# Moving causal convolution taps from VectorE to TensorE in the opening of a mixed Mamba, attention and FFN kernel

## The chip, the cores and the metric

The kernel runs on one core of one Trainium2 chip. The metric is the device time of one execution in microseconds (us). Before the change the median of three executions is 5227.8 us (5223.77 to 5229.38). The core has five engines that run beside each other[...]: TensorE (PE in the profile; PEld is its weight load), VectorE (DVE), ScalarE (ACT), GpSimd (POOL) and SyncE (SP, which here only issues transfers). All data is float32.

## The reference, cut to what matters

The input has 8 batches of 384 channels on a 32 x 32 image, so 1024 positions. Layer 0 is a bidirectional Mamba block with a 3 x 3 depthwise convolution beside it; layer 1 is causal attention and a quantized feed-forward block. The change touches layer 0 alone:

```python
def mamba(x, in_proj_w, conv1d_w, conv1d_b, x_proj_w, dt_proj_w, dt_proj_b, A_log, D_param, out_proj_w):
    xz = jnp.einsum('blc,ec->ble', x, in_proj_w)
    u, z = jnp.split(xz, 2, axis=-1)
    uc = jax.lax.conv_general_dilated(u.transpose(0, 2, 1), conv1d_w[:, None, :], (1,), [(D_CONV - 1, 0)], ...,
                                      feature_group_count=C)          # 4 causal taps, each channel for itself
    u = silu((uc + conv1d_b[None, :, None]).transpose(0, 2, 1))
    x_dbl = jnp.einsum('blc,ec->ble', u, x_proj_w)
    dt, Bm, Cm = jnp.split(x_dbl, [dt_rank, dt_rank + D_STATE], axis=-1)
    delta = jax.nn.softplus(jnp.einsum('blr,dr->bld', dt, dt_proj_w) + dt_proj_b)
    A = -jnp.exp(A_log)
    deltaA = jnp.exp(delta[..., None] * A)
    deltaBu = (delta * u)[..., None] * Bm[:, :, None, :]
    def step(h, inp):
        dA, dBu, c = inp
        h = dA * h + dBu
        return (h, jnp.einsum('bdn,bn->bd', h, c))                    # 16 states for every channel
    _, ys = jax.lax.scan(step, h0, (...))
    y = (ys.transpose(1, 0, 2) + u * D_param) * silu(z)
    return jnp.einsum('bld,od->blo', y, out_proj_w)

fwd = mamba(x_flat, *mparams)
bwd = jnp.flip(mamba(jnp.flip(x_flat, axis=1), *mparams), axis=1)
conv = jax.lax.conv_general_dilated(x_norm, dw_w[:, None, :, :], (1, 1), [(1, 1), (1, 1)], ...)
local_feat = jax.nn.sigmoid(conv + dw_b[None, :, None, None]) * x_norm
x = x + res_scale * ((fwd + bwd) * scale_mod + local_feat)
# layer 1: attention, then a feed-forward block with binarized weights w1, w2
```

## The kernel before

Channels lie on the 128 partitions in three groups `c`; positions lie along a row in two halves `h` of 512. Both directions `d` use the same `up`, the unconvolved projection. Everything of one batch that must be there before the recurrence is made by `before_scan`. It appends small steps to a list `emit`; for the first batch a second list, `later`, takes what the recurrence doesn't need at once.

```python
PARTS = ((0, 0), (0, 1), (1, 1), (1, 0))      # (direction, half), in the order of the recurrence
BANKS = {"y": 1, "da": 2, "s": 2, "pt": 2, "av": 1}      # the 8 banks of PSUM by use
# pools: "big" has 6 buffers of 128 x 3072, "mid" has 10 of 128 x 1024

def before_scan(b, tags, emit, later=None):
    ...                                        # load x, normalize it into st["xn"]
    def in_proj(c, i, h):                      # i = 0: up, i = 1: z
        mp = bank_of(f"in_{b}_{c}_{i}_{h}")
        for k in range(NC):
            nc.tensor.matmul(out=mp, lhsT=st["win", c][:, k, i, :], rhs=st["xn"][:, k, half(h)], ...)   # L337
        nc.scalar.copy(st["up" if i == 0 else "z", c][:, half(h)], mp)                                  # L344

    def conv(c, d, h):
        acc = bank_of(f"u{d}_{b}_{c}_{h}")
        up = st["up", c]
        for s in range(DCONV):
            w = vec[:, c, V_CW + DCONV - 1 - s : V_CW + DCONV - s]
            if s == 0:
                nc.scalar.activation(acc, up[:, half(h)], AF.Copy, scale=w)                             # L353
                continue
            ...                                # tap: up shifted by s, to: where it lands
            nc.vector.scalar_tensor_tensor(to, tap, w, to, ALU.mult, ALU.add)                           # L363
        nc.scalar.activation(st["u", d, c][:, half(h)], acc, AF.Identity, bias=vec[:, c, V_CB : V_CB + 1])  # L364

    def local(c, h): ...                       # 3 x 3 taps: one on ACT (L374), eight on DVE (L384)

    for c in range(NC):
        ...                                    # buffers for up, z and both u; weights of group c + 1
        for i in range(2):
            for h in range(NH):
                emit(lambda c=c, i=i, h=h: in_proj(c, i, h), 2.6)
        for d in range(2):
            for h in range(NH):
                emit(lambda c=c, d=d, h=h: conv(c, d, h), 3.0)
        ...
        if later is None:
            emit(gates, 14.0)                  # silu of both u and of z, local taps, tanh (L384, L424, L443 to L453)
        else:
            emit(gates_of_us, 4.0)             # silu of both u
            later(gates, 10.0)
        ...                                    # project: x_proj on TensorE (L477), summed into xd on DVE (L488)

    def delta(c, d, h):
        ...                                    # softplus: TensorE (L508), four on ACT (L511 to L514)
        nc.vector.scalar_tensor_tensor(dl, dp, 0.0, dl, ALU.max, ALU.add)                               # L515
        nc.vector.scalar_tensor_tensor(dp, w, 1.0, e, ALU.subtract, ALU.subtract)                       # L516
        nc.vector.tensor_tensor(dl, dl, dp, ALU.subtract)                                               # L517
        nc.vector.tensor_tensor(u, u, dl, ALU.mult)                                                     # L518
        ...                                    # both results go to DRAM

    for c in range(NC):
        for d, h in PARTS:
            emit(lambda c=c, d=d, h=h: delta(c, d, h), 3.0)
```

The recurrence is cut into 768 units, 96 for each batch: a part (direction and half), a channel group and two of the 16 states. Within a part the first eight states of groups 0, 1, 2 come first, then the other eight of groups 2, 1, 0. One unit is:

```python
def s_first(u):  # two units ahead
    pin(nc.gpsimd.tensor_tensor(g, ud, bc_row_B, ALU.mult))                          # L578, 128 x 1024
def s_scan(u):
    for i in range(2):
        nc.scalar.activation(da, dl, AF.Exp, scale=amat[:, u.c, n : n + 1])          # L591
        nc.vector.tensor_tensor_scan(gi, da, gi, first, ALU.mult, ALU.add)           # L596
    if begins:
        pin(nc.gpsimd.tensor_copy(carry[:, u.n : u.n + 2], g[:, :, end]))            # L601
    pin(nc.gpsimd.tensor_tensor(g, g, bc_row_C, ALU.mult))                           # L602
def s_sum(u):    # one unit behind: eight 128 x 128 transposes that add up in one bank of PSUM
    nc.tensor.matmul(out=y[:, j, :], lhsT=g[:, i, chunk(j)], rhs=ident, is_transpose=True, ...)  # L610
```

The opening is put together so, with batches in the order 0, 1, 2, 3, 5, 6, 4, 7:

```python
first = slots(-AHEAD - 2, per + 1)             # the recurrence of the first batch
before_scan(ORDER[0], ("s", "pt"), begin, beside)
run(begin)                                     # alone
beside += steps_of(before_scan, ORDER[1], ("s", "pt"))
beside += steps_of(binarize, w1, w1s, NC, FF, 2, "w1")
beside += steps_of(binarize, w2, w2s, NF, C, 8, "w2")
for b in ORDER[2 : 1 + ahead]:                 # the third and fourth batch
    beside += steps_of(before_scan, b, ("s", "pt"))
run(first, beside)                             # spread evenly beside those 96 units
...                                            # then attention and FFN of the batches beside the other units
```

The order in which steps are written is a wish: a scheduler fixes the queue of every engine when the kernel is built, and may move an instruction ahead when it takes its inputs to be ready.

Of the kernel before, what the change touches and what calls it, by code (L numbers as in the profile page):

```python
# [12 lines left out]
ALU = mybir.AluOpType  # L13
# [4 lines left out]
P = 128  # L18
B, C, H, W = 8, 384, 32, 32
L = H * W  # L20
NC = C // P
# [5 lines left out]
DCONV = 4  # L27
# [13 lines left out]
PARTS = ((0, 0), (0, 1), (1, 1), (1, 0))  # L41
# [3 lines left out]
ORDER = (0, 1, 2, 3, 5, 6, 4, 7)  # L45
# [3 lines left out]
V_NORM, V_CW, V_CB, V_DTB, V_D, V_DW, V_DWB, V_BP, V_B2, V_ALOG = 0, 1, 5, 6, 7, 8, 17, 18, 19, 20  # L49
# [4 lines left out]
def kernel(  # L54
# [16 lines left out]
    nc = tc.nc  # L71
# [14 lines left out]
    def btile(name):  # L86
        return big.tile([P, NC, L], F32, name=name, tag="big")

    def mtile(name, n=L):
        return mid.tile([P, n], F32, name=name, tag="mid")  # L90
# [212 lines left out]
                    )  # L303


    def before_scan(b, tags, emit, later=None):

        st = {}
        turns = itertools.cycle(tags)

        def bank_of(name):
            return bank(name, next(turns))
# [19 lines left out]
                    )  # L332

        def in_proj(c, i, h):
            mp = bank_of(f"in_{b}_{c}_{i}_{h}")
            for k in range(NC):
                nc.tensor.matmul(  # L337
                    out=mp,
                    lhsT=st["win", c][:, k, i, :],
                    rhs=st["xn"][:, k, half(h)],  # L340
                    start=(k == 0),
                    stop=(k == NC - 1),
                )
            nc.scalar.copy(st["up" if i == 0 else "z", c][:, half(h)], mp)  # L344

        def conv(c, d, h):

            acc = bank_of(f"u{d}_{b}_{c}_{h}")
            up = st["up", c]
            for s in range(DCONV):  # L350
                w = vec[:, c, V_CW + DCONV - 1 - s : V_CW + DCONV - s]
                if s == 0:
                    nc.scalar.activation(acc, up[:, half(h)], AF.Copy, scale=w)  # L353
                    continue
                lo, hi = h * HB, (h + 1) * HB
                if d == 0:
                    t0, t1 = max(lo, s), hi
                    tap = up[:, t0 - s : t1 - s]
                else:
                    t0, t1 = lo, min(hi, L - s)  # L360
                    tap = up[:, t0 + s : t1 + s]
                to = acc[:, t0 - lo : t1 - lo]
                nc.vector.scalar_tensor_tensor(to, tap, w, to, ALU.mult, ALU.add)  # L363
            nc.scalar.activation(  # L364
                st["u", d, c][:, half(h)], acc, AF.Identity, bias=vec[:, c, V_CB : V_CB + 1]
            )

        def local(c, h):

            acc = bank_of(f"loc_{b}_{c}_{h}")  # L370
            r0, rows = h * (HB // W), HB // W
            img = acc.rearrange("p (i j) -> p i j", j=W)
            src = st["xn"][:, c, :].rearrange("p (i j) -> p i j", j=W)
            nc.scalar.activation(  # L374
                acc, st["xn"][:, c, half(h)], AF.Copy, scale=vec[:, c, V_DW + 4 : V_DW + 5]
            )
            for k in range(9):
                di, dj = k // 3 - 1, k % 3 - 1
                if k == 4:
                    continue  # L380
                i0, i1 = max(r0, -di), min(r0 + rows, H - di)
                j0, j1 = max(0, -dj), W - max(0, dj)
                to = img[:, i0 - r0 : i1 - r0, j0:j1]
                nc.vector.scalar_tensor_tensor(  # L384
                    to,
                    src[:, i0 + di : i1 + di, j0 + dj : j1 + dj],
                    vec[:, c, V_DW + k : V_DW + k + 1],
                    to,
                    ALU.mult,
                    ALU.add,  # L390
                )
            return acc

# [10 lines left out]
        for c in range(NC):  # L404

            @emit
            def _(c=c):
                st["up", c] = mtile(f"up_{b}_{c}")
                st["z", c] = mtile(f"z_{b}_{c}")
                for d in range(2):  # L410
                    st["u", d, c] = mtile(f"u{d}_{b}_{c}")
                if c + 1 < NC:
                    weights_of(c + 1)

            for i in range(2):
                for h in range(NH):
                    emit(lambda c=c, i=i, h=h: in_proj(c, i, h), 2.6)
            for d in range(2):
                for h in range(NH):
                    emit(lambda c=c, d=d, h=h: conv(c, d, h), 3.0)  # L420

            def silus(ts):
                for t in ts:
                    pin(nc.scalar.activation(t, t, AF.Silu))  # L424

            def sum_of_us(c=c):
                usum = mtile(f"us_{b}_{c}")
                nc.vector.tensor_tensor(usum, st["u", 0, c], st["u", 1, c], ALU.add)
                spill((b, "us", c), usum, f"sus_{b}_{c}")
                for d in range(2):  # L430
                    spill((b, "u", d, c), st["u", d, c], f"su_{d}_{b}_{c}")


            def gates(c=c, silus=silus, sum_of_us=sum_of_us):
                st["xc"] = mtile(f"xc_{b}_{c}")
                load(st["xc"], x[b, chunk(c), :])
                accs = [local(c, h) for h in range(NH)]
                with tc.high_priority(offset=60):
                    us = [st["u", 0, c], st["u", 1, c]] if later is None else []
                    silus(us + [st["z", c]])  # L440
                    for h in range(NH):
                        pin(
                            nc.scalar.activation(  # L443
                                accs[h], accs[h], AF.Tanh, scale=0.5, bias=dwbh[:, c : c + 1]
                            )
                        )
                    pin(nc.scalar.preload_act_table_set(LOG_EXP))
                for h in range(NH):
                    acc, xc = accs[h], st["xc"][:, half(h)]
                    nc.vector.scalar_tensor_tensor(  # L450
                        acc, acc, 1.0, st["xn"][:, c, half(h)], ALU.add, ALU.mult
                    )
                    nc.vector.scalar_tensor_tensor(xc, acc, rsh, xc, ALU.mult, ALU.add)  # L453
                spill((b, "t", c), st["xc"], f"st_{b}_{c}")
                spill((b, "z", c), st["z", c], f"sz_{b}_{c}")
                if later is None:
                    sum_of_us()

            def gates_of_us(c=c, silus=silus, sum_of_us=sum_of_us):
                with tc.high_priority(offset=60):  # L460
                    silus([st["u", 0, c], st["u", 1, c]])
                    pin(nc.scalar.preload_act_table_set(LOG_EXP))
                sum_of_us()

            if later is None:
                emit(gates, 14.0)
            else:
                emit(gates_of_us, 4.0)
                later(gates, 10.0)


            for h in range(NH):

                def project(c=c, h=h):
                    xp = bank_of(f"xp_{b}_{c}_{h}")
                    for d in range(2):
                        nc.tensor.matmul(  # L477
                            out=xp[d * DW : (d + 1) * DW, :],
                            lhsT=wx[:, c, :],
                            rhs=st["u", d, c][:, half(h)],  # L480
                            start=True,
                            stop=True,
                        )
                    xd = st["xd"][:, half(h)]
                    if c == 0:
                        nc.scalar.activation(xd, xp, AF.Identity, bias=onerow)
                    else:
                        nc.vector.tensor_tensor(xd, xd, xp, ALU.add)  # L488

                emit(project)  # L490
# [30 lines left out]
                nc.sync.dma_start(out=t, in_=du[:, i, :])  # L521
                spilled[b, what, d, c, h] = t

        for c in range(NC):
            for d, h in PARTS:
                emit(lambda c=c, d=d, h=h: delta(c, d, h), 3.0)


# [560 lines left out]
        for f, _ in spread_over(*lists):  # L1089
            f()  # L1090

    def steps_of(stage, *args):
        out = Steps()
        stage(*args, out)
        return out


# [1 line left out]
    per, ahead = len(units) // B, 3  # L1099
    first = slots(-AHEAD - 2, per + 1)  # L1100
    others = slots(per + 1, len(units) + 1)
    beside = Steps()
    begin = Steps()
    before_scan(ORDER[0], ("s", "pt"), begin, beside)
    run(begin)
    beside += steps_of(before_scan, ORDER[1], ("s", "pt"))
    beside += steps_of(binarize, w1, w1s, NC, FF, 2, "w1")
    beside += steps_of(binarize, w2, w2s, NF, C, 8, "w2")
    for b in ORDER[2 : 1 + ahead]:
        beside += steps_of(before_scan, b, ("s", "pt"))  # L1110
    run(first, beside)

    rest, later, due = [], list(ORDER[1 + ahead :]), [(0.0, 0)]
# [74 lines left out]
```

## Time and profile before

| | us |
|---|---|
| median of three executions | 5227.8 |
| span of the profiled execution | 5226.4 |
| PE busy | 4198.9 (80%) |
| DVE busy | 3630.7 (69%) |
| ACT busy | 2738.5 (52%) |
| POOL busy | 3680.7 (70%) |
| first POOL instruction of the recurrence (L578) starts | 133.90 |
| 192nd scan of 1536 (L596), the last of the first batch, lies between | 815 and 820 |
| last POOL instruction of the recurrence (L602) starts | 4942.6 |

Busy times say how long each engine had something under way, over the whole span. The opening, up to about 815 us, has another mix of work than the rest, and is to be read from its own stretch. The column PEclk is the clock that TensorE was granted, as a share of its full speed[...].

### The profile page before, as it was taken

What the parts mean: (1) busy time and instruction counts of PE and PEld (TensorE: products, weight loads), DVE (VectorE), ACT (ScalarE), POOL (GpSimd) and SP (SyncE); (2) the same over time, 40 slices, a digit from 0 to 9 for tenths busy, and PEclk for the clock granted to TensorE, in tenths of its full rate; (3) what the DMA queues carried; (4) which work ended last, traced back from release to release, by engine and by line L of the source; (5) the groups of instructions that cost most, each with busy time, mean ns of one, the idle gap of its engine ahead of it and who ended that gap; (6) DMA issues with size and microseconds to landing.
All of it is one profiled execution on the core that took longest, in us unless ns stands there. A gap on an engine that the chain in (4) does not pass through costs nothing.

```text
span 5226.4 us, 50586 instructions
## 1 busy us (share of the span) xinstructions
PE 4198.9 (80%) x16554; PEld 2222.6 (43%) x16554; DVE 3630.7 (69%) x4313; ACT 2738.5 (52%) x4934; POOL 3680.7 (70%) x1932
## 2 busy tenths in 40 slices
PE   5455667888878888788887888978888888988799
PEld 2233333444434444444443444434444444544444
DVE  6998998667776667876677856678766655565522
ACT  4665564555644556545556445565464454463334
POOL 0477777887679776787776788677888877787600
PEclk7667677889988899888898889988999989999899
DMA  6544545324463234543244632335433234224200
GB/s 228 210 164 156 184 166 196 109 84 149 143 205 105 91 110 161 169 158 119 97 139 133 213 123 91 108 128 201 141 119 130 89 101 158 85 77 151 83 30 25
DMA packets 365007, 696.35 MB, mean 133 GB/s; under 512 B 30104, under 2 KB 88904, under 8 KB 364744
## 3 DMA queue, kind: packets, MB, share of 16 engines
q1 hardware_dynamic: 355232, 676.97, 38.3%
q10 hardware_dynamic: 9512, 16.15, 0.9%
q8 instruction: 131, 2.15, 0.2%
q14 instruction: 132, 1.08, 0.1%
HBM read 527.33 MB, written 165.68 MB: 133 GB/s over the span
## 4 chain that ended last, share of the span: by engine, by line
POOL 35%; PE 21%; issue 16%; DVE 15%; ACT 4%; DMA 1%; POOLq 0%; SPq 0%; DVEq 0%; ACTq 0%
POOL g L578 18%; POOL g L602 17%; DVE g L596 6%; PE y L610 3%; PE qp L715 3%; PE yp L1015 2%; PE av L854 2%; PE s L770 2%; PE ap L911 2%; DVE loc L384 2%; PE pt L842 1%; DVE dp L516 1%; DVE u L363 1%; PE hp L970 1%; DVE du L518 1%
## 5 line engine op out<-in xcount | busy, mean ns | idle before, releaser
L578 POOL TENSOR_TENSOR g<-ud,bc 128x1024 f32<-128x1024 f32 x768 | 1834.5, 2389 | 730.6 <-PE y L610 579.9
L602 POOL TENSOR_TENSOR g<-g,bc 128x1024 f32<-128x1024 f32 x768 | 1819.8, 2370 | 277.6 <-DVE g L596 215.5
L591 ACT ACTIVATE da<-dl,amat 128x512 f32<-128x512 f32 x1536 | 1057.5, 691 | 1572.1 <-DVE g L596 1530.2
L610 PE MATMUL y<-ident,g 128*128 128x128 f32 x6144 | 969.2, 307 | 403.1 <-POOL g L602 337.6
L596 DVE TENSOR_TENSOR_SCAN g<-da,carry,g 128x512 f32<-128x512 f32 x768 | 954.9, 1271 | 460.2 <-POOL g L578 413.2
L596 DVE TENSOR_TENSOR_SCAN g<-da,g 128x512 f32<-128x512 f32 x768 | 906.5, 1209 | 508.5 <-POOL g L578 483.0
L610 PEld LDWEIGHTS y<-ident,g 128*128 128x128 f32 x6144 | 798.8, 158 | 837.3 <-POOL g L602 504.1
L770 PE MATMUL s<-k,q 64*128 64x512 f32 (+3 forms) x1152 | 469.9, 606 | 166.0 <-ACT pr L790 143.7
L789 DVE TENSOR_REDUCE nm<-s 128x1 f32<-128x512 f32 (+3 forms) x576 | 300.4, 545 | 251.0 <-PE s L779 182.5
L790 ACT ACTIVATE pr<-s,nm 128x512 f32<-128x512 f32 (+3 forms) x576 | 329.4, 575 | 149.5 <-DVE nm L789 148.4
L854 PE MATMUL av<-ptn,v 128*64 128x512 f32 (+3 forms) x1152 | 376.5, 556 | 24.8 <-DVE o L866 24.3
L970 PE MATMUL hp<-t,w 128*128 128x512 f32 x720 | 339.4, 615 | 33.2 <-ACT h L978 10.6
L842 PE MATMUL pt<-ident,pr 128*128 128x128 f32 x1728 | 312.3, 302 | 46.8 <-ACT ptn L844 24.3
L337 PE MATMUL in<-xn,win 128*128 128x512 f32 x576 | 301.2, 665 | 57.2 <-DVE xn L330 16.6
L1015 PE MATMUL yp<-h,w 128*128 128x512 f32 x720 | 330.5, 617 | 10.9 <-DMA w<-w2s 10.9
L844 ACT COPY ptn<-pt 128x512 f32<-128x512 f32 (+3 forms) x576 | 261.8, 480 | 128.8 <-PE pt L842 127.5
L770 PEld LDWEIGHTS s<-k,q 64*128 64x128 f32 x1152 | 163.3, 207 | 332.6 <-ACT pr L790 214.1
L842 PEld LDWEIGHTS pt<-ident,pr 128*128 128x128 f32 x1728 | 209.0, 152 | 180.7 <-ACT ptn L844 82.0
L715 PE MATMUL qp<-t,wqk 128*128 128x512 f32 x576 | 268.0, 616 | 22.0 <-DVE t L301 16.5
L601 POOL COPY carry<-g 128x2 f32<-128x2 f32 x384 | 84.4, 220 | 255.5 <-DVE g L596 255.5
L384 DVE SCALAR_TENSOR_TENSOR loc<-xn,vec,loc 128x496 f32<-128x496 f32 (+3 forms) x384 | 254.6, 721 | 4.3 <-ACT loc L374 4.0
L363 DVE SCALAR_TENSOR_TENSOR u<-up,vec,u 128x512 f32<-128x512 f32 (+3 forms) x288 | 201.5, 743 | 30.8 <-ACT u L353 30.4
(156 smaller groups left out, 4695.0 us busy)
## 6 DMA issues: line engine op xcount, KB each, us to landing
bc<-rows SPq DMA_DIRECT2D x512, 512.0 KB, 4.0
dl<-sdl SPq DMA_DIRECT2D x160, 256.0 KB, 2.8
ud<-sud SPq DMA_DIRECT2D x160, 256.0 KB, 2.7
t<-st SPq DMA_DIRECT2D x63, 512.0 KB, 5.1
su<-u SPq DMA_DIRECT2D x48, 512.0 KB, 5.2
du<-su SPq DMA_DIRECT2D x96, 256.0 KB, 4.5
sdl<-du SPq DMA_DIRECT2D x96, 256.0 KB, 2.7
sud<-du SPq DMA_DIRECT2D x96, 256.0 KB, 2.4
```

The costliest lines, as they stand in the source:

```text
L384: nc.vector.scalar_tensor_tensor(to, src[:, i0 + di : i1 + di, j0 + dj : j1 + dj], vec[:, c, V_DW + k : V_DW + k + 1], to, ALU.mult, ALU.add,)
L578: pin(nc.gpsimd.tensor_tensor(g, ud, sst["bc", 0, u.b, u.part, u.n], ALU.mult))
L591: nc.scalar.activation(da, sst["dl", u.b, u.c, u.part], AF.Exp, scale=amat[:, u.c, n : n + 1])
L596: nc.vector.tensor_tensor_scan(gi[:, ::step], da[:, ::step], gi[:, ::step], first, ALU.mult, ALU.add)
L602: pin(nc.gpsimd.tensor_tensor(g, g, sst["bc", 1, u.b, u.part, u.n], ALU.mult))
L610: nc.tensor.matmul(out=y[:, j, :], lhsT=g[:, i, chunk(j)], rhs=ident, is_transpose=True, start=(u.opens and i == 0 and j == 0), stop=(u.cl ...
L715: nc.tensor.matmul(out=qp, lhsT=st["wqk"][:, c, o : o + P], rhs=st["xn"][:, c, half(h)], start=(c == 0), stop=(c == NC - 1),)
L770: nc.tensor.matmul(out=ss[e][:, : k1 - k0], lhsT=st["q"][rows_of(e), c, chunk(qi)], rhs=st["k"][rows_of(e), c, k0:k1], start=True, stop=(k ...
L842: nc.tensor.transpose(pt[:, chunk(i)], pr[:, e, chunk(j % QT)], ident)
L854: nc.tensor.matmul(out=av[rows_of(e), cols], lhsT=st["v"][:, j, hd * HD : (hd + 1) * HD], rhs=st["ptn", j, e][:, cols], start=(j % QT == 0 ...
L970: nc.tensor.matmul(out=hp, lhsT=st["w1"][:, c, chunk(m % 2)], rhs=st["xn"][:, c, half(h)], start=(c == 0), stop=(c == NC - 1),)
L1015: nc.tensor.matmul(out=yp, lhsT=st["w2", k // 6][:, k % 6, :], rhs=st["h", k // NC][:, k % NC, half(h)], start=(k == 0), stop=(k == NF - 1),)
```

## The change

Three things change, all in the opening. They are for taking work off VectorE while the batches 1, 2 and 3 are prepared beside the first recurrence, and for letting that recurrence begin sooner.

The batches 1, 2 and 3 get their four causal taps as four matmuls that add up in one bank of PSUM. The weight of each is a diagonal matrix with the taps of 128 channels on its diagonal. The twelve diagonals are made once, on GpSimd, from the identity, and lie in one of the six "big" buffers until the last of these convolutions. The first batch and the four later ones (5, 6, 4, 7) keep their taps on ACT and DVE.

The z projections of the first batch go from the part that runs alone to the list beside the recurrence; their weights are held until then, and the buffer of z is taken only when it is made.

The deltas of each batch are made by direction and half first and channel group second, in the order in which the recurrence asks for them.

```diff
-    def before_scan(b, tags, emit, later=None):
+    def before_scan(b, tags, emit, later=None, diags=None):
...
         def in_proj(c, i, h):
+            if i == 1 and h == 0:
+                st["z", c] = mtile(f"z_{b}_{c}")
...
-                w = vec[:, c, V_CW + DCONV - 1 - s : V_CW + DCONV - s]
-                if s == 0:
+                k = V_CW + DCONV - 1 - s
+                w = vec[:, c, k : k + 1]
+                if s == 0 and diags is None:
                     nc.scalar.activation(acc, up[:, half(h)], AF.Copy, scale=w)
                     continue
...
-                nc.vector.scalar_tensor_tensor(to, tap, w, to, ALU.mult, ALU.add)
+                if diags is None:
+                    nc.vector.scalar_tensor_tensor(to, tap, w, to, ALU.mult, ALU.add)
+                else:
+                    nc.tensor.matmul(
+                        out=to,
+                        lhsT=diags(c, k),
+                        rhs=tap,
+                        start=(s == 0),
+                        stop=(s == DCONV - 1),
+                        skip_group_check=True,
+                    )
...
-                st["z", c] = mtile(f"z_{b}_{c}")
...
-            for i in range(2):
+            for i, to in enumerate((emit, emit if later is None else later)):
                 for h in range(NH):
-                    emit(lambda c=c, i=i, h=h: in_proj(c, i, h), 2.6)
+                    to(lambda c=c, i=i, h=h: in_proj(c, i, h), 2.6)
...
-        for c in range(NC):
-            for d, h in PARTS:
+        for d, h in PARTS:
+            for c in range(NC):
                 emit(lambda c=c, d=d, h=h: delta(c, d, h), 3.0)
...
+    taps = btile("taps").rearrange("p c l -> p (c l)")[:, : NC * DCONV * P]
+    taps = taps.rearrange("p (c k q) -> p c k q", c=NC, k=DCONV)
+    for c in range(NC):
+        for k in range(DCONV):
+            nc.gpsimd.tensor_scalar(
+                taps[:, c, k, :], ident, vec[:, c, V_CW + k : V_CW + k + 1], None, ALU.mult
+            )
...
-    beside += steps_of(before_scan, ORDER[1], ("s", "pt"))
+    beside += steps_of(before_scan, ORDER[1], ("s", "pt"), diags=diags)
...
-        beside += steps_of(before_scan, b, ("s", "pt"))
+        beside += steps_of(before_scan, b, ("s", "pt"), diags=diags)
```

More of the change, by code (lines that the diff above doesn't have):

```diff
@@ L383, in local @@
                 to = img[:, i0 - r0 : i1 - r0, j0:j1]
+                tap = src[:, i0 + di : i1 + di, j0 + dj : j1 + dj]
                 nc.vector.scalar_tensor_tensor(
[L385 to L390, printed above, removed]
+                    to, tap, vec[:, c, V_DW + k : V_DW + k + 1], to, ALU.mult, ALU.add
                 )
@@ L1090, in run, with steps_of @@
             f()
-    def steps_of(stage, *args):
+    def steps_of(stage, *args, **kwargs):
         out = Steps()
-        stage(*args, out)
+        stage(*args, out, **kwargs)
         return out
@@ L1101, with diags @@
     others = slots(per + 1, len(units) + 1)
+    taps = btile("taps").rearrange("p c l -> p (c l)")[:, : NC * DCONV * P]
[5 more added lines that the diff above has]
+            )
+    def diags(c, k):
+        return taps[:, c, k - V_CW, :]
     beside = Steps()
```

## The prediction

> **What bounds the kernel now.** I read the stretches first, because the shares of the whole span mix two regimes. I cut the span at four places: the first POOL instruction of the recurrence (133.90 us), the twelfth scan (222 us, at the end of a long wait of POOL), and the 192nd scan (815 us), which ends the first batch. The columns are busy us and count for PE, PEld, DVE, ACT and POOL, then granted clock, DMA share and GB/s.
>
> ```profile
> 0.00:134.00 134.00, 67.22 (x130) 26.43 (x130) 83.77 (x130) 64.56 (x88) 1.44 (x13) 0.73 0.65 229
> ...
> 134.00:222.00 88.00, 30.98 (x66) 14.55 (x67) 86.33 (x111) 51.75 (x75) 34.00 (x18) 0.56 0.60 216
> 222.00:815.00 593.00, 373.66 (x1141) 197.15 (x1139) 542.35 (x636) 368.10 (x549) 429.21 (x221) 0.69 0.51 173
> 815.00:5226.00 4411.00, 3727.07 (x15219) 1984.48 (x15218) 2918.24 (x3438) 2254.10 (x4224) 3216.05 (x1681) 0.90 0.37 123
> ```
>
> From 134 to 815 us DVE is the bound: 86 of 88 us, then 542 of 593 us (91%). From 815 us on it is busy for 66% only and TensorE for 84%, at clock 0.90. What the change takes from DVE can therefore only count in the 593 us; in the 88 us no tap is run.
>
> Next the groups of instructions in 134 to 806 us: busy us and mean ns, then idle time of the engine before them and what ended it.
>
> ```profile
> L578 POOL TENSOR_TENSOR g<-ud,bc 128x1024 f32<-128x1024 f32 x97 | 236.3, 2437 | 132.7 <-DMA sdl<-du 132.0 <-DMA ud<-sud 0.7
> L602 POOL TENSOR_TENSOR g<-g,bc 128x1024 f32<-128x1024 f32 x94 | 222.4, 2366 | 85.9 <-DVE g L596 65.9 <-issue 16.2
> L610 PE MATMUL y<-ident,g 128*128 128x128 f32 x749 | 147.5, 362 | 187.3 <-POOL g L602 185.7 <-DVE yt L629 1.1
> L384 DVE SCALAR_TENSOR_TENSOR loc<-xn,vec,loc 128x465 f32<-128x465 f32 (+3 forms) x192 | 126.1, 720 | 0.1
> L363 DVE SCALAR_TENSOR_TENSOR u<-up,vec,u 128x512 f32<-128x512 f32 (+3 forms) x108 | 75.1, 741 | 1.4 <-ACT u L353 1.2
> L516 DVE SCALAR_TENSOR_TENSOR dp<-ew 128x512 f32<-128x512 f32 x37 | 58.3, 1584 | 0.2
> L353 ACT ACTIVATE u<-up,vec 128x512 f32<-128x512 f32 x36 | 24.1, 682 | 0.0
> ```
>
> The reader sees that the taps never wait (1.4 us before 108 of them), that POOL waits for scans, and that TensorE waits 187 us for POOL: there is room on it. Last the timeline of TensorE at two places, which gives the price of a matmul at either clock.
>
> ```profile
> 430.23 1.02 PE L337 MATMUL in<-xn,win 128*128 128x512 f32 x2
> 433.92 1.09 PE L610 MATMUL y<-ident,g 128*128 128x128 f32 x8 [2.66 <-POOL g L602]
> ...
> 552.01 1.97 PE L610 MATMUL y<-ident,g 128*128 128x128 f32 x8 [2.93 <-POOL g L602]
> ```
>
> [...] the eight transposes of a unit take 1.97 us when they stand alone and 1.09 us behind matmuls, and the opening[...] has clock 0.69 where the rest has 0.90. [...]
>
> **The change part by part.**
>
> Taps off DVE: 108 instructions, 75.1 us busy. A row of them is spaced by 0.67 us (six in 4.02 us), so 72 us are freed. 36 first taps leave ACT, 24.1 us, where 368 of 593 us were busy: nothing for the end.
>
> Taps onto TensorE: 3 batches x 12 accumulators x 4 = 144 matmuls. One float32 matmul is two instructions in this trace (L337 counts 576 for 288), and twelve of them at full clock take 5.15 us (rows of L715 in the chain of waits), 0.43 each. So 144 x 2 x 0.43 = 124 us at full clock. What is there now is 373.66 x 0.69 = 258 us at full clock; the 18 z matmuls of the first batch, which come over, add 18 x 0.86 = 15. Sum 397 us at full clock: 441 us at 0.90, 496 at 0.80, 575 at 0.69, against DVE at 542 - 75 = 467 and POOL at 429. Three engines are then nearly level where one stood out.
>
> Because [...] a unit may run only two or three units ahead, I take the maximum by stretch, not over the whole. One channel group of one batch takes 8 units of the recurrence. Before, on DVE: 12 taps 8.0, 16 local taps 10.2, four more of the gates 2.7, sum of u 1.4, two sums of xd 1.3, 16 scans at 1.23 makes 19.7; together 43.3 us. POOL: 8 x (2 x 2.36 + 0.19) = 39.3 us. TensorE at full clock: four projections 10.3, x_proj 2.7, transposes 8 x 1.09 = 8.7; 21.7 us. DVE bounds it, at 43.3. The stretch of deltas takes 12 x (0.67 + 1.58 + 0.67 + 1.11) = 48 us and 13 scans, 64 us, all DVE. Nine groups and three stretches of deltas give 9 x 43.3 + 3 x 64 = 582 us, with 15 us for normalization 597, against 593 in the trace: the sum holds.
>
> After: DVE 43.3 - 8.0 = 35.3; POOL 39.3; TensorE 21.7 + 16 x 0.86 = 35.5 at full clock, 39.4 at 0.90, 44.4 at 0.80, 51.4 at 0.69. The deltas stay at 64. A group therefore goes from 43.3 to 39.4 at clock 0.90: 9 x 3.9 = 35 us, not 72, because POOL's recurrence stands right below DVE. I choose 0.90 since TensorE will now be busy as densely as in the rest. Of the 35 us I take half, 18 us: where three engines are level, [...] the copy of a finished convolution (L364) stands ahead of the exponentials that the next scans need, and now it waits for TensorE.
>
> z projections: 6 accumulators x 2.57 us leave TensorE before the recurrence, but beside the DVE taps of the same group, not in front of them. Their ACT copies push the third and fourth first tap back, for which DVE waited 0.24 us in the first group. I give it 3 us over three groups.
>
> Order of the deltas: three deltas, not one, are ready when the first unit starts. But from 134 to 222 us DVE is busy for 98%, with all twelve deltas and the local taps of the first batch to do in any order. It brings nothing there by itself. The queues of the changed build also put the sums of w1 ahead of the first normalization, which costs some 6 us at first, and spare the later convolutions the same interleaved sums; I count 2 us in favour over the 134 us. Start: -3 - 2 = -5 us.
>
> The twelve diagonals are 128 x 128 on an idle POOL before 134 us; nothing. The queues after the first 96 units hold the same work in nearly the same order, so the rest keeps its 4411 us and a gain of the opening passes through to the end.
>
> Sum: 5228 - 18 - 5 = 5205 us.
>
> **The rivals.**
>
> TensorE becomes the bound at a low clock. At 0.69 a group would take 51.4 us, 9 x 8.1 = 73 us more than before: 5228 + 73 - 5 = 5296. [...] Against it: the stretch 815 to 5226 us, as dense as this would be, has 0.90.
>
> DVE stays the bound and the whole relief comes through. 75.1 / 0.914 = 82 us: 5228 - 82 - 5 = 5141. For it: DVE's 91% and the taps' idle time of nearly nothing. Against it: 39.3 us of POOL in each group, which a faster DVE cannot go below.
>
> The waits cancel everything. If the ACT queue waits for convolutions, the scans come late and DVE idles where it worked: about 5225. For it: ACT already waited for TensorE before the copies of up (24.0 us in this stretch). Against it: ACT is 62% busy there.
>
> The taps' buffer. One of six big buffers is held, so the image of the third batch may load later. That wait was not on the path, as loads of x were far ahead of their use; some 5 us at the most.
>
> **Range and chances.** The clock carries the range. At 1.00 the group is bound by POOL at 39.3, so 36 us in full and 5 at the start make 5187; a looser tie between POOL and DVE could bring another 20 to 30. At 0.80 a group takes 44.4, 10 us in all against it: 5233, with waits about 5245. So 5160 to 5250 should hold it 8 times in 10. Faster by over 2% needs 105 us, more than the 82 of the second rival and the start together: 0.05. Slower by over 2% needs the low clock and more: 0.03. Within 2%: 0.92.
>
> **What would show it.** Each step has its place in the profile of the changed kernel. The first POOL instruction of the recurrence should start near 129 us. Between the twelfth and the 192nd scan I expect some 575 us in place of 593, with DVE near 470 us busy (about 82%), TensorE near 440 at a clock of about 0.9, POOL still 429. The groups should show 288 matmuls for the taps in place of L363's 108. The time after the 192nd scan should be 4411 us within 20. I am wrong if the clock of that stretch stays near 0.7 (first rival), if DVE is still above 90% busy there (second), if ACT's idle time before the copies of the convolutions exceeds some 40 us (third), or if the time after the first batch changes by more than the opening.

## The result and the profile after

The changed kernel takes 5201.86 us (median of four executions, 5197.06 to 5212.38) against 5225.78 us before (5217.87 to 5229.38). The ratio is 0.9959, with a 95% interval of 0.9939 to 0.9979: 24 us faster, about 0.5%. In a second measurement with 22 executions the ratio is 0.9965 (0.9955 to 0.9975).

First the same stretches as before, cut at the first instruction of the recurrence on GpSimd (129.50 us), at the scan that ends GpSimd's long wait (217.20 us; here it is the ninth, before the change it was the twelfth) and at the first scan of the second batch (808.90 us). The columns are busy us and count for PE, PEld, DVE, ACT and POOL, then granted clock, DMA share and GB/s.

```profile
0.00:129.50 129.50, 52.40 (x94) 19.07 (x94) 83.71 (x131) 61.82 (x82) 8.33 (x24) 0.72 0.65 228
129.50:217.20 87.70, 50.51 (x95) 21.10 (x96) 87.10 (x108) 50.74 (x75) 29.49 (x15) 0.66 0.65 228
217.20:808.90 591.70, 460.70 (x1447) 229.36 (x1445) 486.13 (x543) 357.24 (x525) 443.09 (x227) 0.82 0.52 176
808.90:5195.00 4386.10, 3703.95 (x15208) 1967.51 (x15208) 2910.46 (x3427) 2248.25 (x4217) 3209.95 (x1679) 0.91 0.37 124
```

The prediction put the end of the first batch at 815 us. The last of its scans begins at 819.59 us, and the first of the second batch at 827.42 us, so here is the kernel before once more, from its twelfth scan to the first of the second batch, and below it the changed kernel between the same two scans.

```profile
221.50:827.40 605.90, 380.94 (x1159) 200.79 (x1157) 555.25 (x646) 377.73 (x565) 439.40 (x225) 0.69 0.51 174
220.60:808.87 588.27, 457.85 (x1440) 228.40 (x1440) 482.70 (x540) 355.40 (x522) 442.18 (x226) 0.82 0.52 176
```

VectorE is relieved of 73 us in that stretch (555 to 483) and is now busy for 82% of it in place of 92%. TensorE takes on 77 us at a clock that rises from 0.69 to 0.82. Yet the stretch shrinks by 18 us only. The groups of the changed kernel from 217 to 809 us show where TensorE and GpSimd stand (busy us and mean ns, then idle time before them).

```profile
L587 POOL TENSOR_TENSOR g<-ud,bc 128x1024 f32<-128x1024 f32 x91 | 224.5, 2467 | 26.7 <-PE y L619 26.6
L611 POOL TENSOR_TENSOR g<-g,bc 128x1024 f32<-128x1024 f32 x92 | 218.2, 2372 | 69.1 <-DVE g L605 47.0 <-DMA sud<-du 14.6 <-issue 4.1
L370 PE MATMUL u<-up,taps 128*128 128x512 f32 (+3 forms) x288 | 128.7, 598 | 0.0
L605 DVE TENSOR_TENSOR_SCAN g<-da,carry,g 128x512 f32<-128x512 f32 x96 | 119.2, 1270 | 42.0 <-POOL g L587 37.5 <-ACT da L600 4.4
L605 DVE TENSOR_TENSOR_SCAN g<-da,g 128x512 f32<-128x512 f32 x89 | 104.0, 1208 | 36.1 <-POOL g L587 32.1 <-ACT da L600 4.0
L378 ACT ACTIVATE u<-u,vec 128x512 f32<-128x512 f32 x36 | 23.4, 671 | 0.0
```

The 288 instructions of the taps (L370) cost 128.7 us, and none waits. The copy of a finished convolution (L378) doesn't wait either. What is new stands before the scans: VectorE waits for GpSimd's L587. The view of the waits gives the sum, first of the kernel before (221 to 827 us), then of the kernel after (217 to 809 us): us in total, times, longest.

```profile
POOL carry L601 <- DVE g L596: 115.7, 12, 45.5
POOL g L602 <- DVE g L596: 74.9, 12, 10.4
...
DVE g L596 <- POOL g L578: 12.2, 11, 2.5
```

```profile
POOL carry L610 <- DVE g L605: 99.4, 8, 49.0
DVE g L605 <- POOL g L587: 69.6, 37, 2.5
...
POOL g L611 <- DVE g L605: 47.0, 7, 18.8
```

The longest wait in the first line of either view (45.5 and 49.0 us) is the long one that ends where the stretch begins. VectorE's wait for GpSimd grew from 12.2 to 69.6 us, by 57 us. That is most of the 73 us that it was relieved of. How it looks in time: the timelines of VectorE and of GpSimd in the changed kernel, at the beginning of the preparation of batch 1, where no tap is left on VectorE.

```profile
221.72 2.31 DVE L605 TENSOR_TENSOR_SCAN g<-da,g 128x512 f32<-128x512 f32 x2
224.60 2.34 DVE L605 TENSOR_TENSOR_SCAN g<-da,g 128x512 f32<-128x512 f32 x2 [0.57 <-POOL g L587]
229.47 2.34 DVE L605 TENSOR_TENSOR_SCAN g<-da,g 128x512 f32<-128x512 f32 x2 [2.53 <-POOL g L587]
```

```profile
222.21 2.35 POOL L587 TENSOR_TENSOR g<-ud,bc 128x1024 f32<-128x1024 f32 x1
224.51 0.18 POOL L610 COPY carry<-g 128x2 f32<-128x2 f32 x1
224.77 2.35 POOL L611 TENSOR_TENSOR g<-g,bc 128x1024 f32<-128x1024 f32 x1
227.07 2.36 POOL L587 TENSOR_TENSOR g<-ud,bc 128x1024 f32<-128x1024 f32 x1
229.36 0.20 POOL L610 COPY carry<-g 128x2 f32<-128x2 f32 x1
```

GpSimd works without a gap, 4.87 us for a unit, and VectorE has two scans in that time and nothing else to do. Why it has nothing else to do stands in the timelines of TensorE and ScalarE.

```profile
234.94 3.59 PE L370 MATMUL u<-up,taps 128*128 128x512 f32 x8
240.46 0.69 ACT L600 ACTIVATE da<-dl,amat 128x512 f32<-128x512 f32 x1 [3.07 <-DVE g L605]
...
245.34 0.69 ACT L600 ACTIVATE da<-dl,amat 128x512 f32<-128x512 f32 x1 [3.07 <-DVE g L605]
246.45 0.69 ACT L600 ACTIVATE da<-dl,amat 128x512 f32<-128x512 f32 x1 [0.42 <-DVE g L605]
247.08 0.67 ACT L378 ACTIVATE u<-u,vec 128x512 f32<-128x512 f32 x1
```

The first convolution is finished on TensorE at about 238.5 us. Its copy stands in ScalarE's queue behind exponentials (L600) of the recurrence, which come at GpSimd's pace, and starts only at 247.08 us. ScalarE is idle twice for 3.07 us around that time, until a scan of VectorE ends, and the copy, whose input is finished within the first of these waits, isn't taken ahead of the exponentials.

The pace of a channel group can be read at the instruction that adds both u, one for each group (L428 before, L437 after). Between these additions of one batch lie 43.3 us on average before the change (36.7 to 47.3, six intervals) and 40.2 us after (36.8 to 43.7).

### The profile page after: what moved, and what is told of

Read it like the earlier page. It is cut to its first block, busy times and chain, and to the rows that moved or that the text cites. A ratio compares the mean times of both kernels' runs of the same rounds, so it can differ in the third digit from the quotient of the medians.

```text
span 5195.3 us, 51029 instructions
## 1 busy us (share of the span) xinstructions
PE 4267.6 (82%) x16842; PEld 2237.0 (43%) x16842; DVE 3567.4 (69%) x4205; ACT 2718.1 (52%) x4898; POOL 3690.9 (71%) x1944
## 4 chain that ended last, share of the span: by engine, by line
POOL 38%; PE 20%; DVE 17%; issue 16%; ACT 6%; DMA 3%; POOLq 0%; SPq 0%; ACTq 0%; DVEq 0%
POOL g L587 19%; POOL g L611 18%; DVE g L605 6%; PE qp L724 3%; PE y L619 3%; PE av L863 2%; PE s L779 2%; PE yp L1024 2%; PE ap L920 2%; DVE loc L399 2%; DVE dp L525 2%; PE pt L851 1%; DVE u L368 1%; DVE du L527 1%; PE op L694 1%
## 5 line engine op out<-in xcount | busy, mean ns | idle before, releaser
L587 POOL TENSOR_TENSOR g<-ud,bc 128x1024 f32<-128x1024 f32 x768 | 1837.1, 2392 | 729.7 <-PE y L619 576.5
L600 ACT ACTIVATE da<-dl,amat 128x512 f32<-128x512 f32 x1536 | 1058.6, 692 | 1614.3 <-DVE g L605 1574.0
L619 PE MATMUL y<-ident,g 128*128 128x128 f32 x6144 | 926.1, 298 | 273.6 <-POOL g L611 211.8
L619 PEld LDWEIGHTS y<-ident,g 128*128 128x128 f32 x6144 | 769.4, 153 | 695.3 <-POOL g L611 328.4
L1024 PEld LDWEIGHTS yp<-h,w 128*128 128x128 f32 x720 | 139.7, 198 | 176.9 <-issue 166.4
```

The costliest lines, as they stand in the source:

```text
L587: pin(nc.gpsimd.tensor_tensor(g, ud, sst["bc", 0, u.b, u.part, u.n], ALU.mult))
L600: nc.scalar.activation(da, sst["dl", u.b, u.c, u.part], AF.Exp, scale=amat[:, u.c, n : n + 1])
L1024: nc.tensor.matmul(out=yp, lhsT=st["w2", k // 6][:, k % 6, :], rhs=st["h", k // NC][:, k % NC, half(h)], start=(k == 0), stop=(k == NF - 1),)
```

## The experiments

All ratios are against the kernel before, on the same chip and beside it. The last two columns are read from the traces: when the recurrence starts on GpSimd, and when the second batch's first scan starts.

| run | median us | ratio (95% interval) | start | second batch |
|---|---|---|---|---|
| before (its first profile) | 5225.78 | | 133.9 | 827.4 |
| changed kernel (its first profile) | 5201.86 | 0.9959 (0.9939 to 0.9979) | 129.5 | 808.9 |
| after_again | 5213.26 | 0.9965 (0.9955 to 0.9975) | 128.5 | 804.9 |
| taps_only | 5211.10 | 0.9959 (0.9948 to 0.9970) | 140.1 | 807.5 |
| order_only | 5239.28 | 1.0009 (0.9998 to 1.0019) | 134.1 | 830.4 |
| z_only | 5228.65 | 0.9994 (0.9979 to 1.0008) | 123.9 | 802.7 |
| taps_doubled | 5269.13 | 1.0071 (1.0057 to 1.0085) | 129.0 | 846.4 |
| one_tap | 5212.25 | 0.9956 (0.9939 to 0.9972) | 128.2 | 802.0 |
| deltas_beside_next | 5214.93 | 0.9969 (0.9957 to 0.9981) | 129.3 | 810.1 |
| deltas_and_gates_spread | 5210.59 | 0.9963 (0.9950 to 0.9976) | 129.1 | 807.6 |
| last_deltas_in_rest | 5205.10 | 0.9952 (0.9935 to 0.9968) | 130.0 | 757.5 |
| last_deltas_in_rest_late_gates | 5204.75 | 0.9952 (0.9937 to 0.9967) | 128.7 | 756.8 |
| last_deltas_in_rest_taps_on_vector | 5224.05 | 0.9984 (0.9969 to 0.9998) | 124.5 | 796.7 |
| half_of_second_multiply | 5152.31 | 0.9839 (0.9816 to 0.9862) | 130.5 | 747.4 |

### Which part carries the gain

The first four runs take the change apart. Two theories stood against each other: the gain lies in the taps, or it lies in the start (the z projections and the order of the deltas), for the first 24 units end 20 us earlier in the changed kernel (319 in place of 339 us) than before.

The changed kernel itself, as a yardstick:

> The changed kernel as it is, as a yardstick for the single parts. Both theories: 20 to 30 us under the kernel before, ratio 0.994 to 0.996.

The taps alone. The edit takes back the other two parts:

```diff
-        for d, h in PARTS:
-            for c in range(NC):
+        for c in range(NC):
+            for d, h in PARTS:
                 emit(lambda c=c, d=d, h=h: delta(c, d, h), 3.0)
...
-            for i, to in enumerate((emit, emit if later is None else later)):
+            for i in range(2):
                 for h in range(NH):
-                    to(lambda c=c, i=i, h=h: in_proj(c, i, h), 2.6)
+                    emit(lambda c=c, i=i, h=h: in_proj(c, i, h), 2.6)
```

> The kernel before with the taps of batches 1, 2 and 3 on TensorE and nothing else changed. Theory 1 (the gain lies in the taps, bounded by GpSimd and TensorE): 15 to 22 us under the kernel before; the time between the twelfth scan and the end of the first batch shorter by that much, VectorE near 490 us busy there, TensorE's clock above 0.8. Theory 2 (the gain lies in the start: z and the order of the deltas): within 6 us of the kernel before.

The order of the deltas alone, on the kernel before (the first hunk above, the other way round):

> The kernel before with only the order of the deltas changed. Theory 1: within 4 us of the kernel before, since VectorE is busy for 98% around the first units and has all twelve deltas to do in either order. Theory 2: 8 to 20 us faster, and the first part of the recurrence (24 units) ends some 15 us earlier, as it does in the changed kernel (319 for 339 us).

The z projections alone, on the kernel before (the second hunk, the other way round, with the buffer of z taken when it is made):

> The kernel before with only the z projections of the first batch moved beside the recurrence. Theory 1: 0 to 6 us faster, the first instruction of the recurrence on GpSimd starts 2 to 5 us earlier. Theory 2: 8 to 15 us faster, as TensorE had 15 us of work taken from the part that runs alone.

The taps alone give 0.9959, all that the whole change gives. The order gives nothing that can be told from zero (1.0009, 0.9998 to 1.0019). The z projections start the recurrence 10 us earlier, and the second batch 25 us earlier, and still end at 0.9994 (0.9979 to 1.0008); of the 10 us nothing can be told from zero at the end. Of the 25 us 9 are left at the first scan of the third batch (1396.4 for 1405.6 us). With the taps alone the recurrence starts 6 us later than before: in the queue of VectorE the first normalization now stands behind the sums of w1 and begins at 33.89 us in place of 27.14 (27.04 with z alone). Only with the z projections moved does the recurrence start earlier again. The first theory holds for the times; for z alone it had the start 2 to 5 us earlier, and it was 10.

### How near TensorE is to the bound

Every tap matmul twice, on diagonals of half the weight, which gives the same sum:

```diff
+                    for r in range(2):
-                    nc.tensor.matmul(
-                        ...
-                        start=(s == 0),
-                        stop=(s == DCONV - 1),
+                        nc.tensor.matmul(
+                            ...
+                            start=(s == 0 and r == 0),
+                            stop=(s == DCONV - 1 and r == 1),
...
-                taps[:, c, k, :], ident, vec[:, c, V_CW + k : V_CW + k + 1], None, ALU.mult
+                taps[:, c, k, :], ident, vec[:, c, V_CW + k : V_CW + k + 1], 0.5, ALU.mult, ALU.mult
```

> The changed kernel with every tap matmul done twice on half the weight: the same result, with 288 instead of 144 tap matmuls. Theory 1 (TensorE stands level with GpSimd in the groups of the opening, as the prediction has it): a group then needs 35.5 + 13.8 = 49.3 us of TensorE at full clock, 52 at 0.95, against 43.3 of VectorE before the change; 60 to 110 us slower than the changed kernel and slower than the kernel before. Theory 2 (TensorE has room; VectorE and GpSimd alone set the pace): under 25 us slower than the changed kernel.

One tap matmul in place of four, which leaves three quarters of these convolutions out:

```diff
             for s in range(DCONV):
+                if s > 0 and diags is not None:
+                    continue
...
-                        stop=(s == DCONV - 1),
+                        stop=True,
```

> The changed kernel with one tap matmul in place of four for batches 1, 2 and 3; it leaves three quarters of those convolutions out. Theory 1: with 93 us of matmuls at full clock less, TensorE leaves the bound, the half of the gain that waits took comes back, 10 to 20 us faster than the changed kernel. Theory 2: within 6 us of the changed kernel.

Doubled, the kernel is 0.0106 of the time (55 us) slower than the changed one: near the 60 that the first theory asked for at the least, and far from the second's 25. With a quarter of the matmuls it gains nothing: 0.9956 against 0.9965. A group, read at the additions of both u, takes 49.0 us with doubled taps, which is the 49.3 that the expectation had for TensorE at full clock, and 41.1 with a single tap against 40.2 in the changed kernel. So TensorE is the bound with 288 tap matmuls, and not with 144. The waits say the same. First of the doubled taps (217 to 846 us), then of the single tap (217 to 802 us):

```profile
POOL g L588 <- PE y L620: 108.8, 19, 9.9
DVE g L606 <- POOL g L588: 95.7, 52, 7.0
ACT u L379 <- PE u L371: 49.4, 19, 6.2
```

```profile
DVE g L607 <- POOL g L589: 83.3, 40, 2.5
POOL g L613 <- DVE g L607: 56.1, 9, 11.0
POOL carry L612 <- DVE g L607: 45.1, 6, 14.0
```

With doubled taps GpSimd waits 108.8 us for the transposes of TensorE, which give its buffers back, and ScalarE waits 49.4 us for convolutions. In the changed kernel these are 26.6 us and none. With a single tap they are gone, but VectorE still waits 83.3 us for GpSimd. So it isn't TensorE that keeps the freed time.

### Whether GpSimd keeps it

The second multiply of GpSimd is cut in half for the first batch; half of that product is left out:

```diff
-        pin(nc.gpsimd.tensor_tensor(g, g, sst["bc", 1, u.b, u.part, u.n], ALU.mult))
+        gc, bc = g, sst["bc", 1, u.b, u.part, u.n]
+        if u.b == ORDER[0]:
+            gc, bc = g[:, 0, :], bc[:, 0, :]
+        pin(nc.gpsimd.tensor_tensor(gc, gc, bc, ALU.mult))
```

> The changed kernel with GpSimd's second multiply done for one of the two states of each unit of the first batch only; it leaves half of that product out. It takes some 1.2 us from each of 96 units, 113 us of GpSimd, and leaves the other engines as they are. Theory 1 (where the taps were, VectorE now waits for GpSimd, so GpSimd's pace keeps the freed time): VectorE's wait for GpSimd between the twelfth scan and the end of the first batch falls from 69.6 us below 30, and the first batch ends 20 to 45 us earlier. Theory 2 (other waits between queues hold the time): the wait shrinks, but the first batch ends within 8 us of before.

The second batch starts at 747.4 us, 61 us earlier, and the whole is at 0.9839, so that the gain lasts to the end. Its stretch and its waits from 217 to 747 us:

```profile
217.00:747.00 530.00, 440.54 (x1438) 224.39 (x1438) 464.05 (x536) 353.43 (x521) 343.42 (x226) 0.85 0.59 196
```

```profile
POOL carry L610 <- DVE g L605: 53.6, 11, 18.1
POOL g L614 <- DVE g L605: 50.6, 9, 17.5
DVE g L605 <- POOL g L587: 29.7, 22, 5.6
```

VectorE's wait for GpSimd falls to 29.7 us, under the 30 of the first theory, and the gain is above its 20 to 45 us. VectorE is busy for 88% of the stretch again, and a group takes 37.4 us in place of 40.2. From the ninth scan (210.88 us, 6 us earlier than in the changed kernel) to the first of the second batch it is 536.5 us for 591.6. Of these 55 us, 40 are the wait for GpSimd. The other 15 are VectorE's own busy time, which fell from 486 to 471 us for the same 542 instructions. So GpSimd's pace is what held most of the time that the taps had freed. The same relief was not tried on the kernel before; there VectorE waits for GpSimd for 12.2 us in all, so it had little of that kind to win.

### Whether the rows of deltas can be spread

In the changed kernel GpSimd still waits 146 us for VectorE (99.4 + 47.0, with the long wait of 49.0 at the beginning), in the rows of deltas and local taps. Four runs move that work. First the deltas of batches 1 and 2 beside the preparation of the next batch:

```diff
-            emit(lambda c=c, d=d, h=h: delta(c, d, h), 3.0)
+            (emit if deltas is None else deltas)(lambda c=c, d=d, h=h: delta(c, d, h), 3.0)
...
-    for b in ORDER[2 : 1 + ahead]:
-        beside += steps_of(before_scan, b, ("s", "pt"), diags=diags)
+    for i in range(1, ahead):
+        beside += spread_over(deltas[i - 1], made[i])
+    beside += deltas[ahead - 1]
```

> The changed kernel with the deltas of batch 1 spread beside the preparation of batch 2, and those of batch 2 beside that of batch 3, in place of a row at the end of each; the same work. Theory 1 (the pace is the maximum of the engines stretch by stretch, and the stretches of deltas, all VectorE, are the longest): VectorE work meets TensorE work, 10 to 35 us faster than the changed kernel. Theory 2 (the opening is bound by its sums, or by waits between queues): within 6 us.

Then also the gates, local taps and z projections of the first batch beside the preparation of batch 1:

```diff
-    beside += made[0]
+    beside += spread_over(late, made[0])
```

> As the one before, and the local taps, gates and z projections of the first batch spread beside the preparation of batch 1 in place of ahead of it. This is meant to shorten the wait of 49 us of GpSimd in which VectorE does local taps ahead of the seventh unit's scan. Theory 1: the wait falls below 20 us, and the kernel is another 5 to 20 us faster. Theory 2: the wait goes elsewhere, within 6 us of the run before.

Neither gains at the end. The first one is ahead of the changed kernel by 22 us after 72 units (617.42 for 639.41 us), and by 20 still at the last scan of the first batch (787.47 for 807.09). It loses all of it before the first scan of the second batch (810.09 for 808.87): in these 22 us VectorE works off deltas and makes no scan, since those of batch 2 and batch 3 have come together in this part. Its stretch from 617 to 810 us, with VectorE busy for 93%:

```profile
617.00:810.00 193.00, 146.12 (x450) 71.27 (x450) 180.34 (x196) 131.46 (x189) 128.31 (x55) 0.79 0.60 201
```

In the second one GpSimd's wait of 49 us falls to 12.1 at the longest, and the first 24 units end 12 us earlier again (303.61 for 315.99 us), but by the start of the second batch only 2 us are left.

So the deltas of batch 3 went out of the opening, beside the first steps of the first attention:

```diff
-    beside += deltas[ahead - 1]
+    kept = deltas[ahead - 1]
...
-        rest += steps_of(attention, b, fed) if i < B - 1 else []
+        att = steps_of(attention, b, fed) if i < B - 1 else []
+        if i == 0:
+            att = spread_over(att[:33], kept) + att[33:]
+        rest += att
```

> As the run with the deltas beside the next preparation, and the deltas of batch 3 moved out of the opening, beside the first 33 steps of the first attention. The theory now: the stretches of deltas, which are VectorE alone, keep what the taps have freed; some 45 us of VectorE leave the opening and meet an attention that is bound by TensorE. Theory 1: the first batch ends 30 us or more earlier than in the changed kernel, and 15 to 40 us of it are left at the end, ratio 0.989 to 0.994. Theory 2 (the attention pays for it, being level on TensorE, VectorE and GpSimd too): within 8 us of the changed kernel, ratio 0.995 to 0.998.

> As the one before, with the gates of the first batch spread beside the preparation of batch 1. Theory 1: 3 to 10 us faster than that one. Theory 2: no difference beyond 5 us.

The second batch now starts at 757.5 us, 51 us earlier, and the end doesn't move: 0.9952 against 0.9965, with intervals that overlap. The attention pays. Its first scores begin at 941.06 us, against 933.82 in the changed kernel. The two stretches from 809 to 934 us, the changed kernel first, then the one with the deltas moved there:

```profile
809.00:934.00 125.00, 103.53 (x359) 58.33 (x360) 87.06 (x90) 52.32 (x86) 114.33 (x70) 0.87 0.49 168
```

```profile
809.00:934.00 125.00, 100.61 (x334) 52.35 (x333) 104.93 (x107) 66.14 (x110) 115.09 (x65) 0.89 0.49 162
```

GpSimd is busy for 92% of it in both, and VectorE rises from 70% to 84%. So the deltas lie beside a GpSimd that is nearly full, and the attention begins later though its batch is ahead. But this is not the whole loss: against the first profile of the changed kernel the lead is 33 us at the first scan of the third batch, 22 at the fifth and 2 at the seventh, where two profiles of the changed kernel differ by up to 13. Where the later part goes isn't shown. The late gates add nothing there either.

The last one of these has the taps back on ScalarE and VectorE:

```diff
-        steps_of(before_scan, b, ("s", "pt"), diags=diags, deltas=deltas[i])
+        steps_of(before_scan, b, ("s", "pt"), deltas=deltas[i])
```

> As the run with the last deltas beside the attention, but with the taps of batches 1, 2 and 3 back on ScalarE and VectorE. It tells what the taps on TensorE are worth once the deltas no longer stand in a row. Theory 1: VectorE bounds the opening again nearly everywhere; 25 us or more slower than the same kernel with the taps on TensorE. Theory 2 (the rest or GpSimd bounds all of it): within 12 us of that kernel.

It is 19 us slower than with the taps on TensorE (5224.05 for 5205.10), between the two theories. The taps are worth about the same in both arrangements, so the rows of deltas don't decide what they bring.

## Why the prediction was right, point by point

The bound: VectorE, busy for over 90% of the opening, with the taps as work that never waited. Right. The taps alone give the whole gain.

The size of the relief: 75.1 us of busy time, 72 by spacing. Measured 73. The cost on TensorE, 0.43 us for an instruction at full clock: a row of 16 takes 7.03 us in the trace of the changed kernel, 0.44 each.

The clock in the opening: 0.90 was assumed, 0.82 came. It rose from 0.69, and the first rival (0.69 with a loss of 73 us) is out. But by the prediction's own sum 0.82 means 35.5 / 0.82 = 43.3 us of TensorE for a group, as much as VectorE needed before, and no gain at all. The step that failed is to divide all of TensorE's work by the mean clock of the stretch. In the kernel before, the instructions of L337 start most often 0.43 us after one another (401 times), and next most often 0.85 (51 times). The trace has the granted clock at 1.00 between all of the former and at 0.50 to 0.51 between the latter. Where tap instructions follow one another in the changed kernel, 262 of 266 start 0.43 us after the one before, and the granted clock was 1.00 over 284 of the 288. So the taps ran at full clock, and the lower mean belongs to other times. The eight transposes for which the prediction reads 1.97 and 1.09 us ran at 0.50 (551.9 to 554.1 us) and at 1.00 (433.9 to 435.1 us). That TensorE isn't level with GpSimd in a group is what the run with a single tap shows. That the two errors, the clock and what it costs, left the number right is luck.

The stretch between the twelfth scan and the end of the first batch: 593 to 575 us was expected, 18 us less. Cut at like scans it is 605.9 to 588.3, 18 us less. The step to 35 us rested on GpSimd standing right below VectorE in each group, 43.3 us to 39.4. This is what the runs show: 43.3 us became 40.2, VectorE waits for GpSimd, and wait and group fell when GpSimd was relieved.

The second halving, from 35 to 18 us, has the right size and the wrong reason. It was put down to waits between level engines, with the copy of a finished convolution on ScalarE as the example, which would wait for TensorE ahead of the exponentials. ScalarE is idle for 0.0 us before that copy. With a quarter of the tap matmuls the time is the same, so TensorE doesn't take it either. The traces put the loss in one place. The six intervals between additions of u are 18 us shorter together, and the three pieces with the rows of deltas 14 us. But from the twelfth scan to the first addition of u in batch 1 it is 41.5 us in place of 27.1, 14 us lost. There the copy stands behind the exponentials, as the timelines above show, the work of the group comes late, and VectorE waits for GpSimd with nothing to do. This is read from the timelines, not tried alone; with GpSimd's second multiply halved it is 35.0 us, with a single tap 38.6, so GpSimd's pace has more part in it than TensorE. That half was the right share is luck.

The start: 5 us earlier expected, 4.4 us measured (133.9 to 129.5), and again right for the sum and not for its terms. z alone brings 10 us of earlier start, not 3. The queues of the taps were to bring 2, with 6 us lost at first at the sums of w1 and more won later; the 6 us came, and the taps alone put the start off by 6. The two errors cancel, which is luck. The 0.24 us by which VectorE waited for a first tap said too little of what the z projections hold up. By the end no gain of z alone can be told from zero.

The order of the deltas: nothing expected, nothing found (1.0009).

The rest: 4411 us within 20 was expected. From the second batch on it is 4399 us before, and 4386 and 4407 us in the two profiled executions of the changed kernel, which are 0.6 us apart at 3037 us (batch 5 of the recurrence) and 17 us at the end. So 31 us between the first two profiles are 19 us of the opening and a difference that executions of the same kernel show too.

The second rival, with 82 us for the taps, fails on GpSimd's floor. The third, with nothing, fails on the measured 0.9959. Whether the large buffer of the taps costs anything was not tried alone.

## What to carry to other kernels

VectorE, busy for 92% of a stretch, gave back 18 of the 73 us that were taken from it: first look at what the next engine needs for the same unit of work, here 4.87 us of GpSimd against what VectorE has left, and let only the difference count. After the change, the wait of the relieved engine for the other one (12.2 to 69.6 us) shows where the freed time went, and relieving that other one in an experiment tells it from a mere guess. Don't price added matmuls by the mean clock of a stretch: look at how far apart their starts are in the trace, here 0.43 us at a mean clock of 0.82. Where the work beside a recurrence is moved in time and not removed, judge by the end of the whole, because a batch that ends 51 us earlier may have left its work to the next stage.

## What was not expected of the hardware

The mean granted clock of TensorE in this stretch differed from kernel to kernel: 0.69 with the taps on VectorE, 0.75 with 36 tap matmuls, 0.82 with 144 and 0.88 with 288. TensorE was busy for 63%, 67%, 78% and 87% of the stretch, so the two rose together in these four runs. A tap instruction took 0.57 us of busy time with 36 matmuls (40.9 us for 72 instructions), 0.45 with 144 (128.7 for 288) and 0.43 with 288 (250.5 for 576). The mean clock didn't go with the number of transposes: in the kernel before there are 749 in the 672 us from 134 us on, at clock 0.68, and 5392 in the 4411 us of the rest, at 0.90.

Some instructions of VectorE change their length from kernel to kernel without being changed. Between the long wait and the second batch the second delta instruction (L516, L525) took 1606 ns on average in the kernel before, 1288 in the changed one, and 997 with GpSimd's second multiply cut in half. The sum of both u (L428, L437) took 1595, 2416 and 1763 ns. The first delta instruction stayed at 677, 680 and 680. So with less of GpSimd's work beside them than in the changed kernel the two were shorter by 291 and 653 ns; the fourth delta instruction was not (932 and 981). What lengthened the sum of both u in the changed kernel wasn't tried.
